# Pair products of 32 feature vectors: W packed in one buffer and loaded by halves, chunks aligned at their ends, one transposed-x buffer, x loaded for two tiles at once

## The chip, the cores and the metric

The kernel runs on one core of one Trainium2 chip. The metric is the time of one execution on the device in microseconds (us); the time shown is the median of the runs. The core has a matrix engine (TensorE, PE in the profile), a vector engine (VectorE, DVE), a scalar engine (ScalarE, ACT), GpSimd (POOL) and a sync engine (SyncE, SP), and 16 DMA engines that move data between HBM and the on-chip memory SBUF. TensorE writes its products to PSUM[...].

## The reference

The input has 4096 rows (the batch), each with F = 32 vectors of D = 64 float32 numbers. For each of the 496 pairs i < j, vector i is multiplied with the pair's own 64 x 64 matrix, and the product is multiplied, element by element, with vector j:

```python
i_idx, j_idx = np.triu_indices(32, k=1)
vi = inputs[:, i_idx, :]
vj = inputs[:, j_idx, :]
vdotw = jnp.einsum('bpd,pde->bpe', vi, W)
inter = vdotw * vj
return inter.reshape(B, -1)          # 4096 x 31744, float32: 520 MB
```

The input is 33.6 MB and the matrices are 8.1 MB, so nearly all traffic to HBM is output.

## The kernel before

A tile is 128 rows of the batch, one on each SBUF partition; there are NT = 32 tiles, and the outer loop runs over them. Inside a tile, the features i are taken two at a time: pair p stands for features 2p and 2p+1, h = 0 or 1 says which. The rows of x are transposed on TensorE (`transpose_x`, line 97), eight 128 x 128 blocks at a time into two PSUM banks, and copied by ScalarE into xT (line 103). In xT the 64 numbers of feature 2p lie on partitions 0 to 63 and those of feature 2p+1 on partitions 64 to 127. W is laid out likewise: the matrices of even features are in the lower 64 partitions, those of odd features in the upper 64. A product with one feature (line 145) uses 64 partitions of xT and W.

All products of feature i with W are (31 - i) x 64 columns wide, which is `width[i]`. They are computed in chunks of up to 512 columns, counted from the row's beginning. One chunk takes two banks, one for the even and one for the odd feature. VectorE then multiplies both banks with x in one instruction (line 155), or each by itself where the ends of the rows don't fit (line 164). The result goes into `ring`, a buffer of 28160 columns in SBUF. A tile has four groups of pairs, and after each group SyncE issues one store of its columns (line 170):

```python
STORES = [[0, 1], [2, 3], [4, 5, 6], [7, 8, 9, 10, 11, 12, 13, 14, 15]]
PREFETCH_AT = [5, 6]
RING = 28160
```

The groups have 7552, 6528, 7872 and 9792 columns, so a whole tile (31744) doesn't fit into the ring, and a group writes where an earlier store has lain; it has to wait until that store has left.

There are two x buffers, used in turn. At the start of tile t, ScalarE's queue issues the load of tile t+1 (lines 82 and 125), and at pairs 5 and 6 of tile t the two halves of tile t+1 are transposed into the other one of two xT buffers (line 136). W is loaded once, at the start, by 16 DMAs on SyncE's queue, one for each pair, over all 128 partitions (line 115). The odd feature's row is 64 columns shorter than the even one's and is padded with zeros, so that both have one width. The stores are in the same queue behind the loads of W. The order of instructions is that of the program text; the tile framework adds the waits.

Of the kernel before, what the change touches and what calls it, by code (L numbers as in the profile page):

```python
# [1 line left out]

# [6 lines left out]

F32 = mybir.dt.float32  # L10
ALU = mybir.AluOpType

P = 128
BANK = 512
BANKS = 8
CHUNK = BANK

STORES = [[0, 1], [2, 3], [4, 5, 6], [7, 8, 9, 10, 11, 12, 13, 14, 15]]
PREFETCH_AT = [5, 6]
RING = 28160  # L20


@with_exitstack
def pair_bilinear_kernel(
    ctx: ExitStack,
    tc: tile.TileContext,
    x: bass.AP,
    w: bass.AP,
    out: bass.AP,
    F: int,  # L30
    D: int,
):

    nc = tc.nc
    B = x.shape[0]
    NT = B // P
    NPR = F // 2

    width = [(F - 1 - i) * D for i in range(F)]
    off = [sum(width[:i]) for i in range(F)]
    woff = [sum(width[0 : 2 * p : 2]) for p in range(NPR)]  # L60
    store_w = [sum(width[2 * p] + width[2 * p + 1] for p in g) for g in STORES]

    const = ctx.enter_context(tc.tile_pool(name="const", bufs=1))
    xtpool = ctx.enter_context(tc.tile_pool(name="xT", bufs=2))
    psum = ctx.enter_context(tc.tile_pool(name="ps", bufs=1, space=bass.MemoryType.PSUM))

    ident = const.tile([P, P], F32, tag="ident", name="ident")
    make_identity(nc, ident)

    def runs(tl, a, b, n):  # L70

        ap = tl[:, a : a + n]
        return bass.AP(ap.tensor, ap.offset, [list(ap.ap[0]), [b - a, 2], list(ap.ap[1])])


    xbuf = [const.tile([P, (F + 1) * D], F32, tag=f"x{b}", name=f"x{b}") for b in range(2)]
    for xb in xbuf:
        nc.gpsimd.memset(xb[:, F * D :], 0.0)  # L78

    def load_x(t):  # L80
        xt = xbuf[t % 2]
        nc.scalar.dma_start(out=xt[:, : F * D], in_=x[ts(t, P), :])
        return xt

    pring = psum.tile([P, BANKS * BANK], F32, tag="pring", name="pring")
    bank = 0

    def take_banks(n):

        nonlocal bank  # L90
        if bank + n > BANKS:
            bank = 0
        got = pring[:, bank * BANK : (bank + n) * BANK]
        bank = (bank + n) % BANKS
        return got

    def transpose_x(xT, t, xt, g):

        n = 2 * BANK // P
        pt = take_banks(2)  # L100
        for c in range(n):
            nc.tensor.transpose(pt[:, ts(c, P)], xt[:, ts(n * g + c, P)], ident)  # L102
        nc.scalar.copy(xT[:, ts(g, 2 * BANK)], pt)  # L103

    def new_xT(t):
        return xtpool.tile([P, NPR * P], F32, tag="xT", name=f"xT_{t}")

    ring = const.tile([P, RING], F32, tag="ring", name="ring")
    at = 0
    xs = {0: load_x(0)}  # L110

    w_sb = []
    for p in range(NPR):
        wp = const.tile([P, width[2 * p]], F32, tag=f"w{p}", name=f"w{p}")
        nc.sync.dma_start(out=wp, in_=w[:, woff[p] : woff[p] + width[2 * p]])
        w_sb.append(wp)

    xTs = {0: new_xT(0)}
    for g in range(2):
        transpose_x(xTs[0], 0, xs[0], g)  # L120

    for t in range(NT):
        xt, xT = xs.pop(t), xTs.pop(t)
        if t + 1 < NT:
            xs[t + 1] = load_x(t + 1)
        for s, group in enumerate(STORES):
            if at + store_w[s] > RING:
                at = 0
            osb = ring[:, at : at + store_w[s]]
            at += store_w[s]  # L130
            o0 = off[2 * group[0]]
            for p in group:
                if t + 1 < NT and p in PREFETCH_AT:
                    if t + 1 not in xTs:
                        xTs[t + 1] = new_xT(t + 1)
                    transpose_x(xTs[t + 1], t + 1, xs[t + 1], PREFETCH_AT.index(p))
                for c0 in range(0, width[2 * p], CHUNK):
                    n = [max(0, min(CHUNK, width[2 * p + h] - c0)) for h in range(2)]
                    half = -(-n[0] // BANK) * BANK
                    pm = take_banks(2 * half // BANK)  # L140
                    for b0 in range(0, n[0], BANK):
                        b1 = min(b0 + BANK, n[0])
                        for h in range(2):
                            if b0 < n[h]:
                                nc.tensor.matmul(  # L145
                                    pm[:, h * half + b0 : h * half + b1],
                                    xT[h * D : (h + 1) * D, ts(p, P)],
                                    w_sb[p][h * D : (h + 1) * D, c0 + b0 : c0 + b1],
                                    start=True,
                                    stop=True,  # L150
                                )
                    o = [off[2 * p + h] - o0 + c0 for h in range(2)]
                    xj = [(2 * p + h + 1) * D + c0 for h in range(2)]
                    if n[1] > half - BANK and o[1] + n[0] <= store_w[s]:
                        nc.vector.tensor_tensor(  # L155
                            runs(osb, o[0], o[1], n[0]),
                            runs(pm, 0, half, n[0]),
                            runs(xt, xj[0], xj[1], n[0]),
                            ALU.mult,
                        )  # L160
                    else:
                        for h in range(2):
                            if n[h]:
                                nc.vector.tensor_tensor(  # L164
                                    osb[:, o[h] : o[h] + n[h]],
                                    pm[:, h * half : h * half + n[h]],
                                    xt[:, xj[h] : xj[h] + n[h]],
                                    ALU.mult,
                                )
            nc.sync.dma_start(out=out[ts(t, P), o0 : o0 + store_w[s]], in_=osb)  # L170


# [33 lines left out]
```

## Time and profile before

| | |
|---|---|
| Median of 3 runs | 1337.88 us (1337.68 to 1337.98) |
| The profiled execution | 1337.58 us |
| Its span, first to last instruction | 1335.8 us |
| VectorE busy | 1199.1 us (90%), 1344 instructions |
| TensorE busy | 1154.1 us (86%), 5376 products; weight loads 529.9 us |
| ScalarE busy | 66.1 us (5%) |
| DMA | 562.88 MB in 25403 packets, mean 421 GB/s |
| HBM | 41.94 MB read, 520.09 MB written |

The table has times of busy engines, summed over the span. Engines work side by side, so the sums don't add up to the span. The profile calls a line of the kernel L and its number, "out<-in" names the buffers that an instruction writes and reads, and an arrow before an engine's name says what the idle time was waiting for. q1 is the DMA queue of SyncE and q10 that of ScalarE.

### The profile page before, as it was taken

The page shows a single profiled execution, that of the slowest core. Times are in us where ns is not written, and L with a number is a line of the kernel's source. Part 1 is how long each engine was busy: PE and PEld are TensorE (multiplying, and loading weights), DVE is VectorE, ACT ScalarE, POOL GpSimd, SP SyncE. Part 2 cuts the span into 40 slices and gives each one's busy share as a digit, 9 for nine tenths or more (in the row PEclk, how much of TensorE's full clock was granted, in tenths as well). Part 3 has the DMA queues.
Part 4 walks back from the last instruction along what each step waited for, and adds up shares of the span by engine and source line. Part 5 has one row for each costly group of instructions (what it writes and reads, how often), then busy time and mean ns, then how long its engine had stood idle before and what let it go on. Part 6 is the DMA issues. An engine that isn't in the chain of part 4 may idle for free. (4 is left out here: it accounts for less than half of the span.)

```text
span 1335.8 us, 13084 instructions
## 1 busy us (share of the span) xinstructions
PE 1154.1 (86%) x5376; PEld 529.9 (40%) x5376; DVE 1199.1 (90%) x1344; ACT 66.1 (5%) x65; POOL 0.9 (0%) x8
## 2 busy tenths in 40 slices
PE   7898898988888889898888898898988888888883
PEld 3343343433343444344334444343443333333331
DVE  5999898999899999899999899989988989999994
ACT  1000000000000000000000000000000000000000
POOL 0000000000000000000000000000000000000000
PEclk9999999899999999999999999999999999999997
DMA  9999999999999999999999999999999999999998
GB/s 392 435 426 431 436 408 434 415 426 431 419 417 425 428 429 416 418 424 420 424 436 419 418 421 426 424 426 421 418 430 414 426 423 413 424 427 430 418 420 370
DMA packets 25403, 562.88 MB, mean 421 GB/s; under 512 B 2944, under 2 KB 3328, under 8 KB 4864
## 3 DMA queue, kind: packets, MB, share of 16 engines
q1 hardware_dynamic: 20736, 528.49, 92.6%
q10 hardware_dynamic: 4608, 33.56, 6.0%
q8 instruction: 42, 0.69, 0.2%
q14 instruction: 17, 0.14, 0.0%
HBM read 41.94 MB, written 520.09 MB: 421 GB/s over the span
## 5 line engine op out<-in xcount | busy, mean ns | idle before, releaser
L155 DVE TENSOR_TENSOR ring<-pring,x 128x1024 f32<-128x1024 f32 (+3 forms) x1088 | 1154.2, 1107 | 116.9 <-DMA out_dram<-ring 68.0
L145 PE MATMUL pring<-w,xT 64*128 64x512 f32 (+4 forms) x4864 | 1087.8, 563 | 132.3 <-DVE ring L155 127.9
L145 PEld LDWEIGHTS pring<-w,xT 64*128 64x128 f32 x4864 | 472.9, 192 | 721.4 <-DVE ring L155 611.7
L103 ACT COPY xT<-pring 128x1024 f32<-128x1024 f32 x64 | 64.8, 1012 | 1197.1 <-PE pring L102 1197.1
L102 PE MATMUL pring<-ident,x 128*128 128x128 f32 x512 | 71.5, 285 | 30.7 <-DMA x<-in_x_dram 30.3
L102 PEld LDWEIGHTS pring<-ident,x 128*128 128x128 f32 x512 | 57.0, 144 | 65.6 <-issue 65.6
L164 DVE TENSOR_TENSOR ring<-pring,x 128x64 f32<-128x64 f32 (+4 forms) x256 | 70.9, 297 | 3.3
L103 ACT ACT_TABLE_LOAD x1 | 1.3, 1283 | 1.7 <-PEq L198 1.7
masks.py:199 POOL TENSOR_SCALAR_AFFINE_SELECT ident<-ident 128x128 f32<-128x128 f32 x1 | 0.3, 292 | 0.0
L78 POOL MEMSET x<- 128x64 f32 x2 | 0.2, 152 | 0.0
masks.py:197 POOL MEMSET ident<- 128x128 f32 x1 | 0.2, 204 | 0.3 <-POOLq L198 0.3
L198 POOL MEMSET const-bfloat16-1.0<- 128x1 bf16 x1 | 0.1, 101 | 0.0
L198 POOL MEMSET const-uint8-127<- 128x1 uint8 x1 | 0.1, 101 | 0.0
L198 POOL MEMSET const-float32-0.0<- 128x1 f32 x1 | 0.1, 98 | 0.2 <-issue 0.2
L198 POOL MEMSET const-float32-1.0<- 128x1 f32 x1 | 0.1, 98 | 0.0
## 6 DMA issues: line engine op xcount, KB each, us to landing
out_dram<-ring SPq DMA_DIRECT2D x32, 4896.0 KB, 18.6
out_dram<-ring SPq DMA_DIRECT2D x32, 3936.0 KB, 17.4
out_dram<-ring SPq DMA_DIRECT2D x32, 3776.0 KB, 19.0
out_dram<-ring SPq DMA_DIRECT2D x32, 3264.0 KB, 19.4
x<-in_x_dram ACTq DMA_DIRECT2D x32, 1024.0 KB, 17.8
w<-in_w_dram SPq DMA_DIRECT2D x1, 992.0 KB, 7.5
w<-in_w_dram SPq DMA_DIRECT2D x1, 928.0 KB, 11.8
w<-in_w_dram SPq DMA_DIRECT2D x1, 864.0 KB, 13.4
```

Of the source, the lines that this page charges most:

```text
L78: nc.gpsimd.memset(xb[:, F * D :], 0.0)
L102: nc.tensor.transpose(pt[:, ts(c, P)], xt[:, ts(n * g + c, P)], ident)
L103: nc.scalar.copy(xT[:, ts(g, 2 * BANK)], pt)
L145: nc.tensor.matmul(pm[:, h * half + b0 : h * half + b1], xT[h * D : (h + 1) * D, ts(p, P)], w_sb[p][h * D : (h + 1) * D, c0 + b0 : c0 + b1 ...
L155: nc.vector.tensor_tensor(runs(osb, o[0], o[1], n[0]), runs(pm, 0, half, n[0]), runs(xt, xj[0], xj[1], n[0]), ALU.mult,)
L164: nc.vector.tensor_tensor(osb[:, o[h] : o[h] + n[h]], pm[:, h * half : h * half + n[h]], xt[:, xj[h] : xj[h] + n[h]], ALU.mult,)
L198: nc = bacc.Bacc("TRN2", target_bir_lowering=False, num_devices=1)
```

## The change

- **W** is one buffer of 16384 columns. It is loaded by ten DMAs instead of 16: the pairs are put into five groups (`LOADS`), and each group is loaded by two DMAs, one over partitions 0 to 63 (even features) and one over partitions 64 to 127 (odd features). In the upper half the odd features' rows follow each other without padding, shifted by 64 columns, so that the ends of both rows of a pair lie at the same column.
- **Chunks** are counted from the row's end: the first chunk of a row has the remainder, all others 512 columns. Both features of a pair then have the same columns j in a chunk, and one range of x, read twice, serves both (a stride of 0). Where the row has only one chunk, the two features are multiplied by an instruction each.
- **xT** is one buffer. Its first half is filled for tile t+1 at pair 9 of tile t, its second half for tile t at pair 3 of tile t itself.
- **x** has one buffer with three slots. Tile 0 is loaded by itself, then the tiles in twos by one DMA each, the last alone. The host lays out x in the order of loads, so that a load of two tiles is one row of 16 KB on each partition. The padding column block of x and its two memsets are gone.
- **Rows of the batch**: partition p now holds rows 32p to 32p+31, one for each tile. The output is addressed as 128 rows of 32 x 31744 numbers, so neighbouring partitions of one store are 4,063,232 bytes apart instead of 126,976.

Stores, ring and the number of products are the same.

```diff
-CHUNK = BANK
-PREFETCH_AT = [5, 6]
+LOADS = [[0], [1], [2, 3], [4, 5, 6], [7, 8, 9, 10, 11, 12, 13, 14, 15]]
+FIRST_HALF_AT, SECOND_HALF_AT = 9, 3
...
+def x_slots(NT):
+    loads = [[(0, 0)]]
+    for t in range(1, NT, 2):
+        if t + 1 == NT:
+            loads.append([(t, 1)])
+        elif loads[-1][-1] == (t - 1, 2):
+            loads.append([(t + 1, 0), (t, 1)])
+        else:
+            loads.append([(t, 1), (t + 1, 2)])
+    return loads
...
-    woff = [sum(width[0 : 2 * p : 2]) for p in range(NPR)]
+    woff = [i % 2 * D + sum(width[i % 2 : i : 2]) for i in range(F)]
...
-    xbuf = [const.tile([P, (F + 1) * D], F32, tag=f"x{b}", name=f"x{b}") for b in range(2)]
-    for xb in xbuf:
-        nc.gpsimd.memset(xb[:, F * D :], 0.0)
-    def load_x(t):
-        xt = xbuf[t % 2]
-        nc.scalar.dma_start(out=xt[:, : F * D], in_=x[ts(t, P), :])
-        return xt
+    xbuf = const.tile([P, 3 * F * D], F32, tag="x", name="x")
+    x_loads = x_slots(NT)
+    slot = {t: xbuf[:, ts(s, F * D)] for load in x_loads for t, s in load}
+    def load_x(load):
+        at = sum(len(before) for before in x_loads[: x_loads.index(load)]) * P * F * D
+        n = len(load) * F * D
+        s = load[0][1]
+        nc.scalar.dma_start(
+            out=xbuf[:, s * F * D : s * F * D + n],
+            in_=x[at : at + P * n].rearrange("(p c) -> p c", p=P),
+        )
...
-    w_sb = []
-    for p in range(NPR):
-        wp = const.tile([P, width[2 * p]], F32, tag=f"w{p}", name=f"w{p}")
-        nc.sync.dma_start(out=wp, in_=w[:, woff[p] : woff[p] + width[2 * p]])
-        w_sb.append(wp)
-    xTs = {0: new_xT(0)}
-    for g in range(2):
-        transpose_x(xTs[0], 0, xs[0], g)
+    xT = const.tile([P, NPR * P], F32, tag="xT", name="xT")
+    load_x(x_loads[0])
+    w_sb = const.tile([P, sum(width[0::2])], F32, tag="w", name="w")
+    for g in LOADS:
+        for h in range(2):
+            a = woff[2 * g[0] + h]
+            b = woff[2 * g[-1] + h] + width[2 * g[-1] + h]
+            if h and g is LOADS[0]:
+                a -= D
+            nc.sync.dma_start(
+                out=w_sb[h * D : (h + 1) * D, a:b], in_=w[h * D : (h + 1) * D, a:b]
+            )
+    transpose_x(slot[0], 0)
     for t in range(NT):
...
+        xt = slot[t]
+        for load in x_loads:
+            if min(load)[0] == t + 1:
+                load_x(load)
...
+                if p == SECOND_HALF_AT:
+                    transpose_x(xt, 1)
+                if p == FIRST_HALF_AT and t + 1 < NT:
+                    transpose_x(slot[t + 1], 0)
+                first = (width[2 * p] - 1) % BANK + 1
+                for c1 in range(first, width[2 * p] + 1, BANK):
+                    n = first if c1 == first else BANK
+                    c0 = c1 - n
+                    odd = width[2 * p + 1] and c1 > D
...
+                    xj = xt[:, (2 * p + 1) * D + c0 : (2 * p + 1) * D + c1]
+                    o = [off[2 * p + h] - o0 + c0 - h * D for h in range(2)]
+                    if odd and (c0 or c1 < width[2 * p]):
+                        nc.vector.tensor_tensor(
+                            runs(osb, o[0], o[1], n),
+                            runs(pm, 0, BANK, n),
+                            bass.AP(xj.tensor, xj.offset, [xj.ap[0], [0, 2], xj.ap[1]]),
+                            ALU.mult,
+                        )
...
-            nc.sync.dma_start(out=out[ts(t, P), o0 : o0 + store_w[s]], in_=osb)
+            nc.sync.dma_start(
+                out=out[:, t * cols + o0 : t * cols + o0 + store_w[s]], in_=osb
+            )
```

## The prediction

> **What bounds the kernel now.** I read the utilisation page first, then the stretches, the waits and the timeline of one tile. The page already names the resource:
>
> ```profile
> DMA  9999999999999999999999999999999999999998
> ...
> DMA packets 25403, 562.88 MB, mean 421 GB/s; under 512 B 2944, under 2 KB 3328, under 8 KB 4864
> ...
> q1 hardware_dynamic: 20736, 528.49, 92.6%
> q10 hardware_dynamic: 4608, 33.56, 6.0%
> ```
>
> Stores and W (q1) and x (q10) fill 98.6% of the 16 DMA engines' span. The busy time in stretches shows when this begins:
>
> ```profile
> 0.00:2.00 2.00, 0.00 (x0) 0.00 (x0) 0.00 (x0) 0.35 (x1) 0.88 (x8) 1.00 0.39 52
> ...
> 5.00:10.00 5.00, 1.46 (x7) 1.49 (x8) 0.00 (x0) 0.00 (x0) 0.00 (x0) 1.00 1.00 424
> 10.00:15.00 5.00, 5.00 (x23) 3.25 (x23) 1.39 (x2) 2.02 (x2) 0.00 (x0) 1.00 1.01 423
> ...
> 30.00:110.00 80.00, 71.80 (x340) 33.12 (x340) 74.83 (x84) 4.05 (x4) 0.00 (x0) 0.98 1.00 431
> 110.00:1300.00 1190.00, 1047.56 (x4884) 480.98 (x4884) 1089.62 (x1221) 58.70 (x58) 0.00 (x0) 0.98 0.99 423
> ```
>
> The last two columns are the DMA share and GB/s. DMA is full from 5 us on, loads first, then stores. So a microsecond added to the loads at the start moves everything after it: there is no idle DMA time later to catch it up. VectorE is second (1199.1 us busy). Of the waits (total us, times, longest) its main one is for DMA:
>
> ```profile
> DVE ring L155 <- DMA out_dram<-ring: 68.0, 35, 3.0
> ```
>
> and the timeline of VectorE around one such wait:
>
> ```profile
> 599.74 0.21 DVE L164 TENSOR_TENSOR ring<-pring,x 128x64 f32<-128x64 f32 x1
> 602.47 9.00 DVE L155 TENSOR_TENSOR ring<-pring,x 128x1024 f32<-128x1024 f32 x8 [2.51 <-DMA out_dram<-ring]
> ```
>
> VectorE stops about 2.5 us a tile (start of store group 2) until an old store has left the ring; consecutive such waits end at 561.45, 602.47 and 643.35, so a tile takes 41 us, of which VectorE uses 38.5. The share of 0.99 after 110 us is worth a look: the trace's packet records show that most DMA engines run dry for about 0.5 us before a tile's fourth store, while one engine finishes each store about 3 us after the others (I infer engines from packets whose starts and ends join) and never runs dry. That slowest engine sets the 41 us, so VectorE has about 3 us per tile to lose before it runs dry too.
>
> W's 16 loads today:
>
> ```profile
> 0.74 22.97 SPq L115 DMA_DIRECT2D w<-in_w_dram  x16
> ...
> 24.68 27.78 SPq L170 DMA_DIRECT2D out_dram<-ring  x4
> ```
>
> The last W load is issued at 23.4 us and lands 5.4 us later (row w 32.0 KB), so loads end near 28.8 us. Bytes agree: 8.389 MB of W and two x tiles (2.097 MB) at 0.424 MB/us are 24.7 us, after a start at 2.3 and before a landing delay of about 1.
>
> [...]No DMA of the kernel before touches fewer than 128 partitions[...].
> [...]in the records an 8 KB x packet (309 ns) follows each store packet while x is being loaded.
> [...]The trace has only a pitch of 126,976 B for stores.
>
> **The change part by part.**
>
> *W in halves: the large term.* W goes from 16 loads of 128 partitions to 10 of 64 (five groups, each half by itself). Bytes: 16,384 columns in the lower and 15,424 in the upper half, x 64 partitions x 4 B = 8.143 MB, 0.246 MB less, because most padding isn't loaded; at 0.424 that saves 0.6 us. [...]I take half of the trace's rate, 0.212 MB/us (an estimate[...]). W alone: 8.143/0.212 = 38.4 us; at full rate it would be 19.2: **+19.2 us** on the path. The first three x tiles (3.146 MB, 7.4 us at 0.424) alternate with W packets. Up to the last load: 2.3 + 38.4 + 7.4 = 48.1 us, instead of 2.3 + 26.6 = 28.9. Lower bound: if lower and upper halves overlapped fully across engines, [...]the cost is nothing. I don't take that: the two halves of a group follow each other in one queue, in the same order on every engine.[...]
>
> Do stores then wait for VectorE? Cumulated the same way, W group 0 lands near 11 us, 1 near 20, [2, 3] near 28, [4, 5, 6] near 37.5, the last near 49. Group by group VectorE takes about 8.4, 7.8, 9.5 and 12.6 us (its own timeline), so the stores are issued near 25, 37 and 49 us; they queue behind W in SP's queue and DMA takes them from 48 to 74.6 us (stores 0 to 2 hold 21,952 columns, x 512 B = 11.24 MB at 0.424). The fourth group writes where stores 0 and 1 lay, so it waits for store 0 to land (48 + 9.1 + 1 = 58) and is issued near 71, just in time for 74.6. So the delay is not made worse, and nothing takes it back.
>
> *Queue positions.* SP issues six W loads at once; later ones wait for earlier transfers (the last for the first pair of x, near 20 us), while DMA still has W packets. Stores stand behind, as before. Nothing.
>
> *x in pairs.* 17 loads instead of 32, rows of 16 KB instead of 8 KB. Store packet medians (968 ns at 26,112 B, 1448 at 39,168) give 36.8 ns per 1000 B plus 8 ns for each packet. x packets fall from 4096 to 2176, W's from 2048 to 640: 3328 x 8 ns / 16 = 1.7 us. Completion packets (9 ns): 21 fewer DMAs x 16 x 9 / 16 = 0.2. Together with the 0.6 above: **-2.4 us**. x lands in about 17 to 20 us either way, every second tile holds up store 3 by 2.5 us more and the next by 2.5 less; VectorE's 3 us cover it. Loads wait for the tile before last or earlier, on ACT's queue, as today; behind them stand only the copies to xT.
>
> *One xT, transposes at pairs 9 and 3.* The first half is overwritten after pair 9 begins, when TensorE has already read pairs 0 to 7; the second likewise. TensorE's own order covers it, so no new wait; copies (1.0 us) have about 10 us before their use. The waits of L102 for x (30.3 us, 8.5 of it at the start) mostly vanish, but hold up nobody at the bound. At the start 8 transposes instead of 16 precede the first product: 1.8 us earlier, hidden because W now comes later.
>
> *Chunks aligned at their ends.* Per tile 43 VectorE instructions instead of 42. Group 0 merges 320 and 256 (480 + 411 ns) into 640 (818): -73. Group 2 merges 192 and 128 (347 + 279) into 384 (550): -76. Group 3 splits 896, 640 and 384 (1079, 818, 550) into 448+384, 320+256, 192+128 (about 617 + 548, 891, 626): +236. Net +87 ns, 2.8 us per run, inside VectorE's 3 us per tile. If that cover were gone: +2.8. One x range read twice replaces two ranges; no row shows it, and I bound it by -2 and +2% of 38 us, less than the cover. Matmul and copy counts stay.
>
> *Output and x layouts.* Stores keep their sizes; the stride between partitions grows from 126,976 to 4,063,232 B (32 rows). Price taken: none[...].
>
> **Sum.** The profiled execution took 1337.58 us (span 1335.8), 0.30 below the median of 1337.88. 1337.58 + 19.2 - 2.4 = 1354.4; moved to the median, **1354.7**.
>
> **Rivals.**
> - *The halves cost nothing* (not slower): engines run at their own rate[...] or drift until both halves are in flight. [...]Only -2.4 remains: 1335.5. It decides if W's last load lands before about 31 us.
> - *Half overlap*: x packets push engines apart, so both halves are partly in flight together. About half of 19.2: 1345.
> - *Row pitch*: [...]520.1 MB at 0.424 are 1227 us[...]. It would show in stores after 100 us[...].
>
> **How the numbers follow.** Main case 0.64 (own range 1349 to 1360), half overlap 0.14 (1338 to 1349), nothing 0.12 (1333 to 1338), pitch 0.10. A measurement here tells about 0.2%, 2.7 us, from no change; the nothing case lies at -2.4, so I split it into faster 0.05 and same 0.07. Slower 0.88. Range 1335 to 1361: it leaves out the pitch case and the edges.
>
> **What would show it.** Right: GB/s near 210 to 300 between 5 and 45 us; W's last landing near 49; first store's bytes after 48; from 110 us on the same 423 GB/s and 41 us per tile; the L155 waits on DMA much as now. Wrong: 420 GB/s during the loads; or stores slower in mid-run; or VectorE without DMA waits, which would make it the bound.

## The result, and the profile after

The changed kernel takes **1355.93 us** (median of 4 runs, 1354.47 to 1358.67) against 1337.78 us: a ratio of 1.0138, with a 95% interval of 1.0119 to 1.0156, or 18.15 us more. The forecast was 1354.7. The profiled execution took 1358.67 us, the longest of the four; its span is 1356.9 us.

The busy time in stretches of the changed kernel tells where the time went (columns: stretch, length, busy us and instructions of PE, PEld, DVE, ACT, POOL, TensorE's clock, DMA share, GB/s):

```profile
2.00:5.00 3.00, 0.00 (x0) 0.00 (x0) 0.00 (x0) 0.90 (x1) 0.00 (x0) 1.00 0.84 338
5.00:50.00 45.00, 30.89 (x116) 18.24 (x116) 23.37 (x24) 2.02 (x2) 0.00 (x0) 0.92 1.03 225
50.00:110.00 60.00, 51.14 (x228) 23.85 (x227) 48.82 (x57) 3.04 (x3) 0.00 (x0) 0.91 1.00 428
110.00:1300.00 1190.00, 1048.10 (x4877) 489.64 (x4877) 1072.84 (x1250) 58.72 (x58) 0.00 (x0) 0.96 0.99 424
```

From 5 to 50 us the DMA engines are as busy as ever (share 1.03), but move 225 GB/s instead of 424. This is the trap in the share column: a packet counts as busy time for as long as it takes, however slowly its bytes move. From 50 us on, the rates are those of the kernel before (431 and 423 then, 428 and 424 now).

The answer for the line of W's loads (durations of issuing, first and last start), and the timeline of SyncE's queue, date the end of the loads:

```profile
L144 SPq DMA_DIRECT2D w<-in_w_dram x10: 465/588/698, 0.7 to 20.1; - x10
```

```profile
0.73 19.96 SPq L144 DMA_DIRECT2D w<-in_w_dram  x10
30.86 21.76 SPq L197 DMA_DIRECT2D out_dram<-ring  x3
```

The last load is issued at 20.1 us, and the page's DMA issues give its time to landing:

```profile
w<-in_w_dram SPq DMA_DIRECT2D x1, 1152.0 KB, 32.5
```

so W is complete at 52.6 us, instead of 28.8. The first store's packets start at 51.1 us in the packet records (the middle of the 16 engines), against 27.8 before. In the same records a W packet of 20,736 bytes takes 1616 ns, a store packet of 26,112 bytes 968: 12.8 against 27.0 bytes per ns, on the same 16 engines.

The totals of the DMA queues and the waits of VectorE:

```profile
q1 hardware_dynamic: 19232, 528.25, 92.6%
q10 hardware_dynamic: 2448, 33.56, 6.1%
```

```profile
DVE ring L183 <- DMA out_dram<-ring: 106.0, 43, 6.7
DVE ring L183 <- PE pring L173: 29.2, 12, 21.5
```

Packets fell as expected (25,344 to 21,680 in these two queues). VectorE's first instruction waits 21.5 us (13.6 before) for the first products, which wait for W. Less expected is that VectorE waits longer for stores than before, 106.0 us instead of 68.0. Its timeline shows these waits to come in turns:

```profile
625.94 9.07 DVE L183 TENSOR_TENSOR ring<-pring,x 128x896 f32<-128x896 f32 x9 [6.15 <-DMA out_dram<-ring]
...
664.48 9.07 DVE L183 TENSOR_TENSOR ring<-pring,x 128x896 f32<-128x896 f32 x9 [1.32 <-DMA out_dram<-ring]
```

The wait before store group 2 is 6.15 us in one tile, in which two tiles of x are loaded, and 1.32 in the next, in which none is. From 625.94 to the start of the next wait, 664.48 - 1.32 = 663.16, are 37.2 us of VectorE's own time for a tile. Before it was 38.5. VectorE has become faster, which the prediction had the other way round.

### The profile page after: what moved, and what is told of

Its sections match the earlier page's. It is cut to its first block, busy times and chain, and to the rows that moved or that the text cites. A ratio compares the mean times of both kernels' runs of the same rounds, so it can differ in the third digit from the quotient of the medians.

```text
span 1356.9 us, 13084 instructions
## 1 busy us (share of the span) xinstructions
PE 1164.7 (86%) x5376; PEld 546.7 (40%) x5376; DVE 1183.2 (87%) x1376; ACT 66.1 (5%) x65; POOL 0.7 (0%) x6
## 4 chain that ended last, share of the span: by engine, by line
DMA 47%; DVE 38%; issue 10%; PE 4%; DVEq 0%; SPq 0%
DMA out_dram<-ring 45%; DVE ring L183 32%; DVE ring L191 6%; PE pring L173 4%; DMA w<-in_w_dram 1%; DVEq L183 0%; PE pring L130 0%; SPq L144 0%; DVEq L228 0%; DVEq L191 0%
## 5 line engine op out<-in xcount | busy, mean ns | idle before, releaser
L173 PE MATMUL pring<-w,xT 64*128 64x512 f32 (+4 forms) x4864 | 1101.8, 564 | 166.1 <-DVE ring L183 135.9
L183 DVE TENSOR_TENSOR ring<-pring,x 128x1024 f32<-128x1024 f32 (+3 forms) x1056 | 1104.2, 1107 | 146.0 <-DMA out_dram<-ring 106.0
L173 PEld LDWEIGHTS pring<-w,xT 64*128 64x128 f32 x4864 | 490.4, 192 | 734.2 <-DVE ring L183 527.6
L191 DVE TENSOR_TENSOR ring<-pring,x 128x64 f32<-128x64 f32 (+3 forms) x320 | 97.6, 355 | 9.9 <-DMA out_dram<-ring 9.2
## 6 DMA issues: line engine op xcount, KB each, us to landing
out_dram<-ring SPq DMA_DIRECT2D x32, 3264.0 KB, 19.1
```

The source lines that it names most:

```text
L173: nc.tensor.matmul(pm[:, h * BANK : h * BANK + n], xT[h * D : (h + 1) * D, ts(p, P)], w_sb[h * D : (h + 1) * D, a : a + n], start=True, st ...
L183: nc.vector.tensor_tensor(runs(osb, o[0], o[1], n), runs(pm, 0, BANK, n), bass.AP(xj.tensor, xj.offset, [xj.ap[0], [0, 2], xj.ap[1]]), ALU ...
L191: nc.vector.tensor_tensor(osb[:, o[h] + h * D : o[h] + n], pm[:, h * (BANK + D) : h * BANK + n], xj[:, h * D :], ALU.mult,)
```

## The experiments

### The halves: taken away, and done alone

One edit of the changed kernel: the same number of W loads, cut by columns instead of partitions.

```diff
-        for h in range(2):
-            a = woff[2 * g[0] + h]
-            b = woff[2 * g[-1] + h] + width[2 * g[-1] + h]
...
-            nc.sync.dma_start(
-                out=w_sb[h * D : (h + 1) * D, a:b], in_=w[h * D : (h + 1) * D, a:b]
-            )
+        a = woff[2 * g[0]]
+        b = woff[2 * g[-1]] + width[2 * g[-1]]
+        m = a + (b - a) // 2 // D * D
+        for lo, hi in ((a, m), (m, b)):
+            nc.sync.dma_start(out=w_sb[:, lo:hi], in_=w[:, lo:hi])
```

> The changed kernel, with W loaded by ten DMAs as before in number, but each over all 128 partitions (each group's columns cut in two instead of its partitions; 0.246 MB of padding is loaded again). Theory[...]: loads return to about 424 GB/s, the last W load lands near 30 us instead of 52.9, and the time is 1337.8 - 2.4 + 0.6, about 1336. Rival (something else in the change costs the 18 us: grouping, waits at the start, chunks, the row stride of the stores): stays at 1352 or more.

Measured: 1337.14 us (1337.02 to 1337.58), ratio to before 0.9995 (0.9987 to 1.0004). The stretches of this kernel are back at the full rate:

```profile
15.00:20.00 5.00, 4.91 (x28) 2.39 (x26) 5.00 (x6) 0.00 (x0) 0.00 (x0) 1.00 1.02 424
20.00:25.00 5.00, 4.79 (x24) 2.06 (x22) 5.00 (x6) 0.91 (x1) 0.00 (x0) 1.00 1.02 424
```

So 18.8 us of the changed kernel's time are the cut by partitions, though the expected 1336 was not quite reached. Everything else in the change, taken together, moves the time by 0.7 us here. Then the counterpart, the cut alone in the kernel before:

```diff
-        nc.sync.dma_start(out=wp, in_=w[:, woff[p] : woff[p] + width[2 * p]])
+        for h in range(2):
+            nc.sync.dma_start(
+                out=wp[h * D : (h + 1) * D],
+                in_=w[h * D : (h + 1) * D, woff[p] : woff[p] + width[2 * p]],
+            )
```

> The kernel before, with one edit: each of the 16 W loads is split into a load of partitions 0 to 63 and one of 64 to 127. Theory: W takes twice as long, 8.389/0.212 instead of 8.389/0.424, +19.8 us: about 1357.5 (1354 to 1361). Rival (the halves cost nothing by themselves): 1338 to 1340, for 16 more DMAs.

Measured: 1356.89 us (1356.24 to 1358.3), ratio 1.0144 (1.0129 to 1.0159): 19.1 us more, where 19.8 was worked out. Its loads run at half rate too:

```profile
5.00:45.00 40.00, 33.49 (x142) 17.50 (x144) 25.52 (x27) 4.05 (x4) 0.00 (x0) 0.91 1.02 230
```

The cut is sufficient and necessary for the loss. That the halves cost nothing is ruled out. The runs show what the cut costs (W's packets moved at 216 GB/s in the changed kernel, 8.143 MB in 37.6 us of packets on an engine in the mean), not what it does inside the chip.

### Both halves in flight from two queues

The changed kernel with `(nc.scalar if h else nc.sync).dma_start` for W: packets for the lower and the upper partitions now come from two queues, and in the packet records both kinds are moving for most of the load, though from 37 us on only the upper ones are left.

> The changed kernel, with the upper halves of W issued on ScalarE's queue and the lower ones on SyncE's[...]. Theory A ([...]alternating doesn't help): 1352 to 1357. Theory B[...]: loads near 400 GB/s, 1337 to 1342[...].

Measured: 1351.96 us (1351.71 to 1352.29), ratio 1.0105 (1.0088 to 1.0122). This is just below theory A's range and far from theory B. The loads are hardly faster:

```profile
5.00:40.00 35.00, 24.65 (x110) 11.53 (x110) 20.78 (x21) 3.31 (x3) 0.00 (x0) 1.00 1.02 236
```

With two queues the loads stay far below the 424 GB/s of loads over 128 partitions; why was not shown. Where the 4.0 us against the changed kernel come from can be read in the packet records of the profiled executions. The table has the summed time of the packets before the first store, divided by 16 engines, and when that store begins:

| us | W's packets | x's packets | first store |
|---|---|---|---|
| W in five loads of 128 partitions (below) | 20.8 | 7.4 | 30.1 |
| the changed kernel | 37.6 | 11.8 | 51.1 |
| halves from two queues | 35.2 | 3.2 | 40.3 |

Two things differ. The load of x's first pair came after W here, because it stood behind W's loads in ScalarE's queue. In the changed kernel it comes amid W, and its 16 KB packets take 1087 ns in the mean instead of 613 later; with 8 of them on each engine, 8 x 0.474 = 3.8 us. And W's own packets take 2.4 us less (8.143 MB at 231 GB/s instead of 216). Together they are 6.2 us, and these two profiled executions are 6.4 us apart (1358.67 and 1352.29), more than the medians. How much each gave to the 4.0 us of the medians stays open, and so does how the records share out time between an x packet and the W packets around it.

### The row stride of the stores

The kernel before, with the changed kernel's assignment of rows to partitions and its output addressing; x is arranged on the host for one tile at a time.

```diff
-            nc.sync.dma_start(out=out[ts(t, P), o0 : o0 + store_w[s]], in_=osb)
+            nc.sync.dma_start(
+                out=out[:, t * cols + o0 : t * cols + o0 + store_w[s]], in_=osb
+            )
```

> The kernel before, with the changed kernel's rows of the batch: partition p has rows 32p to 32p+31, stores go to rows 4,063,232 bytes apart; x is laid out on the host for loads of one tile. Theory (the stride is free): 1337.8 within 0.5. Rival (a small cost of the stride hides the gain from the larger x packets in mid-run): 1339 or more.[...]

Measured: 1337.82 us against 1337.83, ratio 1.0000 (0.9991 to 1.0008). A stride of 4,063,232 bytes costs nothing here.

### The rest of the change, and x in pairs

The first experiment with one load for each group instead of two (five in all), and the same with `x_slots` returning `[[(t, t % 3)] for t in range(NT)]`, so that x is loaded for one tile at a time.

> The changed kernel with W loaded by five DMAs over all 128 partitions, one for each group. All of the change but the halves. By the prediction's small terms -2.4 + 0.6 for the padding, about 1336.0; the ten loads of 128 partitions gave 1337.14, and five fewer DMAs with 640 fewer packets should give at most 0.5 less. If it stays at 1337 the -2.4 was too large by about one.

> The same as the kernel with five W loads, but x is loaded for one tile at a time (32 DMAs with rows of 8 KB, three slots in turn). Theory (8 ns for each packet that is saved, on every engine): 1.1 us slower than with loads of two tiles. Rival (the larger x packets bring nothing, because the slowest DMA engine's time or the alternation of heavy and light tiles takes it back): no slower, within 0.3, or faster.

Measured: five loads 1336.81 us (1336.54 to 1336.93), ratio 0.9992 (0.9983 to 1.0000); x one tile at a time 1337.91 (1337.72 to 1338.02), ratio 1.0000 (0.9992 to 1.0008), with 1337.90 for the kernel before. The pairs of x are worth 1.10 us, as was worked out from 8 ns a packet and the completion packets of 15 loads, 9 ns each (1.1). The rest of the change (fewer and larger W packets, aligned chunks, one xT, stride) comes to nothing in sum. The five loads with x in pairs are the fastest version that ran, 1.09 us below the kernel before, 0.08%, at the edge of what can be told.

### How much VectorE time is free

If DMA bounds, VectorE may lose some time without a cost. The kernel before, with the first product of pair 7 repeated in every tile:

```diff
-                        nc.vector.tensor_tensor(
+                        for _ in range(3 if (p, c0) == (7, 0) else 1):
+                            nc.vector.tensor_tensor(
```

with 3 for two redundant products, 6 for five, 2 for one.

> The kernel before, with one redundant VectorE product of 2 x 512 columns repeated in each tile's last store group (same values, 1.2 us; 38.9 us of VectorE work more in all). Theory (the slowest DMA engine sets the tile's 41 us; VectorE has 2.5 to 3 us a tile to lose): no change, 1337.8 within 1. Rival (VectorE, the ring and the stores form one loop, and the engines that run dry show it): every us counts, up to 1376.

The kernel that ran has two redundant products, where this text says one. The following texts count right.

> The same with five redundant products (6.1 us a tile). Theory: VectorE needs 38.5 + 6.1 = 44.6 us a tile, 3.6 over the 41, so about 30 x 3.6 = 108 us more: 1430 to 1460, and the waits of VectorE for DMA go to nearly nothing. Rival (one loop): 32 x 6.1 = 195 more, 1530.

> The kernel before with really one redundant product of 2 x 512 columns in each tile's last group (the kernel called e6_vec1 has two, although the text sent with it says one). It adds about 1.13 us and one wait for VectorE's own write (0.19) to a tile. Theory (slack of about 2.4 us a tile, the wait at store group 2): 1337.8 to 1340. Rival (time grows from the first added microsecond, at the rate of the two products: 22 us for 2.7 us a tile): about 1348.

| redundant products a tile | time, us | more than before, us | ratio (95%) |
|---|---|---|---|
| one | 1338.88 | 1.0 | 1.0007 (0.9998 to 1.0015) |
| two | 1360.01 | 22.1 | 1.0172 (1.0148 to 1.0196) |
| five (2 runs) | 1472.45 | 134.5 | 1.1006 (1.0986 to 1.1026) |

One product is nearly free, as its theory had it (1337.8 to 1340), and in its timeline the wait at store group 2 has shrunk from 2.4 or 2.5 us to about 1:

```profile
644.60 9.01 DVE L156 TENSOR_TENSOR ring<-pring,x 128x1024 f32<-128x1024 f32 x8 [1.19 <-DMA out_dram<-ring]
```

Two cost 0.7 us a tile; the expectation of no change failed. In that trace group 3 is 2.4 us longer than before in the mean of tiles 4 to 29, and 0.5 us of it are waits for TensorE, which the kernel before does not have there:

```profile
630.81 4.55 DVE L156 TENSOR_TENSOR ring<-pring,x 128x896 f32<-128x896 f32 x5 [1.09 <-PE pring L145]
```

So the slack is about 1.5 us a tile, where 3 were claimed: of the 2.3 us of two products 0.7 were paid, of the 5.7 us of five 4.2. Past it time grows almost one for one: from two to five products, 3 x 1.13 x 32 = 108 us of VectorE work cost 112. The five products lie 12 us above the range of their theory and 58 us below the rival, for which every added microsecond counts.

The same two products in the version with five W loads, with x in pairs and one tile at a time:

> The changed kernel with W in five loads of 128 partitions, and two redundant products a tile as in e6_vec1 (about 2.6 us). The wait at store group 2 alternates here between 6.1 and 1.3 us, as x comes in pairs. Theory A (the mean wait, 3.7 us, is what counts): no change, 1336.8 to 1339. Theory B (the tile with the short wait counts): 16 x 1.3 = 21 more, 1358. Without the faster VectorE of the aligned chunks it would be as in the kernel before, where two products cost 22 us.

> The same with x loaded for one tile at a time; the wait at store group 2 is 3.7 us in every tile. Theory (the aligned chunks take 1.3 us of VectorE's time a tile away, which is slack as long as DMA bounds): two products fit, 1337.9 to 1340. Rival (the aligned chunks give VectorE nothing): 1360, as two products cost in the kernel before.

Measured: pairs 1371.32 us, 34.5 more than without the two products; one at a time 1349.38, 11.5 more. Theory B fits the pairs better than theory A, but its size was too small (21). One at a time, the result lies between theory (1340) and rival (1360), and the cost is half of the 22.1 in the kernel before. That fits the time which the aligned chunks give VectorE, though this version differs from the kernel before in more than the chunks; here too the waits for TensorE grow, from under 0.1 to 0.4 us a tile. The stretch from 110 us on for pairs and two products shows DMA no longer full:

```profile
110.00:1300.00 1190.00, 1061.00 (x4742) 513.83 (x4740) 1104.57 (x1268) 56.67 (x56) 0.00 (x0) 0.95 0.97 411
```

## Why the prediction was right, and where its terms were off

**W in halves** was the whole of it, as predicted: +19.2 us worked out, 19.1 measured between the changed kernel and its twin with five loads of 128 partitions (1355.93 - 1336.81), which loads 0.6 us of padding more. The mechanism, W at half rate and no idle DMA time to catch it up, is shown, but that the two numbers meet so closely is in part luck. In the profiled executions of these two kernels, 21.8 us apart, W's packets account for 16.8 us and x's for another 4.4, which the prediction put at nothing. W at half rate was right (38.4 us worked out, 37.6 measured); W at full rate was taken as 19.2 and is 20.8 with the padding. The price, half of the 0.424 MB/us in the trace, was the author's estimate, as no DMA of the kernel before covers fewer than 128 partitions; W's packets alone then moved at 216 GB/s. From two queues they moved at 231, 7% more.

**The end of the loads** was put near 49 us and came at 52.6. The term at fault is the 7.4 us for x at full rate: x's packets took 11.8 us, 3.8 of the excess in the first pair. Nearly all of the pair's packets were slowed, 109 of 128 to over 1000 ns, so it is not only those for the half that W is filling at the time; why is open. The stores were issued at 30.9, 43.3 and 52.3 us instead of near 25, 37 and 49, since the first group of W was complete only at 19.6 us instead of 11. That cost nothing, as DMA came to the first store only at 51.1 us.

**That nothing gives the time back** held. From the start of the fourth tile's last store to that of the thirtieth tile, the packet records give 1065.5 us, against 1065.3 before.

**The small gains, -2.4 us,** were too large. The pairs of x brought their 1.1. Leaving the padding out was not tried by itself. For W's fewer packets and DMAs 0.8 was claimed; the kernel with five loads and single x has them and stands at 1337.91 against 1337.90. In the traces W's packets do take 0.45 us less there (20.8 instead of 21.3 on each engine). What takes this back stays open; it is 0.03%.

**The aligned chunks** were priced at +87 ns a tile from mean durations, and measured 1.3 us less (38.5 to 37.2). The step at fault is that durations were summed where starts count. In the kernel before, the last chunk of a row writes 64 padding columns which the next row's first instruction overwrites, and in the trace that instruction is released by VectorE's own write, after a gap of about 104 ns. From one start to the next, an instruction of 384 columns takes 650 ns before and 465 after, one of 896 columns 1183 and 1008, though each lasts as long as ever (550 and 548 ns for 384). A tile had ten of these stops and now has three, where a row has only two chunks; seven stops of about 185 ns make 1.3 us. The gain doesn't show in the time, since DMA bounds.

**x in pairs "covered by VectorE's 3 us"** was right for this kernel, but with less left over than claimed: the tiles in which no x is loaded wait 1.1 to 1.3 us, and two products cost three times as much as with single loads.

**The rivals.** No cost of the halves: ruled out from both sides. Half overlap through drifting engines (1345): not seen, W's packets stayed at 216 GB/s. The row stride: free, 1337.82 us with 4,063,232 bytes against 1337.83 with 126,976.

## What to carry to other kernels

Look at the partitions of a DMA before its bytes: here the same matrices took nearly twice as long (37.6 us against 20.8) when each load covered 64 partitions, while the share of busy DMA engines stayed at 1.0 and only the GB/s column told of it. Because DMA is full to the end of this run, the slower start was paid in full. And before you count on an engine's slack, look at its shortest wait, not the mean: grouping two tiles' loads saved 1.1 us of DMA, and made the slack uneven.

## What the runs showed of the hardware that was not expected

- An x packet of 16 KB slowed from 613 to 1087 ns beside W's half loads, although x's loads cover all 128 partitions, and nearly all of its packets did so.
- Splitting the halves over two queues raised the rate of W's packets only from 216 to 231 GB/s.
- VectorE's wait for its own preceding write cost about 185 ns each time (384 columns: 650 ns from start to start instead of 465), in gaps so short that the waits of the kernel before list only 0.9 us of them.
